# Attention normalizations, residual, input sums and chunk sums on GpSimd, and 29 mixed experts in 16 slots

## The chip, the cores and the metric

The kernel runs on one core of one Trainium2 chip. The metric is the time of one execution on the device, in microseconds (us); smaller is better. Before the change the median of three runs is 3224.7 us (3222.76 to 3225.04).

A core has five engines, each with an instruction stream that it takes in order: TensorE (PE: matrix products and transposes; its weight loads are listed as PEld), VectorE (DVE), ScalarE (ACT), GpSimd (POOL) and SyncE (SP, which in this kernel issues all data transfers). They wait for each other by semaphores. PE writes to PSUM, a small memory of eight banks that DVE and ACT read. In this kernel GpSimd works on SBUF alone, the larger on-chip memory.

## What is computed

Two layers over x of shape (4, 2048, 512), all in float32: a windowed attention (16 heads of width 32; a window of 128 queries looks at the keys of the window before, its own and the one after), then a feed-forward layer whose weights are mixed from 8 experts, one mix for each of the 4 sequences. Cut to what matters:

```python
x = x + layernorm(attention(layernorm(x), w_qkv))
x = x + layernorm(ffn(layernorm(x), ...))

def ffn(x):                                        # E = 8 experts, F = 2048, H = 512
    h = relu(einsum('bsh,oh->bso', x, gate_w1) + gate_b1)
    g = (einsum('bso,eo->bse', h, gate_w2) + gate_b2).mean(axis=1)
    mW1 = W1 + einsum('be,efh->bfh', g, TW1)       # the mixing
    mW2 = W2 + einsum('be,ehf->bhf', g, TW2)
    mb1, mb2 = b1 + g @ Tb1, b2 + g @ Tb2
    u = gelu(einsum('bsh,bfh->bsf', x, mW1) + mb1[:, None, :])
    return einsum('bsf,bhf->bsh', u, mW2) + mb2[:, None, :]
```

The gate g of a sequence is a mean over the whole sequence, so its weights can be mixed only when the attention has passed all of it.

## The kernel before

The order of all work is written out by hand; no scheduler moves anything. There are two stages.

**Attention.** 64 windows (W_) of 128 rows, 4 groups of heads (g) for each: 256 slots, slot i being window i // 4, group i % 4. A block K is four windows, 512 rows. One slot issues, in this order (the loop at line 962):

- `scores(i + 1)`: 8 products of q and k (L649) for the slot after, and on DVE two reductions for the negated row maxima `nm` (L658);
- `turn(i, j)`: 12 transposes of the probabilities `pr` on PE (L686), copied out of PSUM by ACT to `prT` (L691). The banks for them (`ptp`) are three that rotate under the tag "pt"; whatever transposes come next (`pto`, `ptx`) take the bank that the first copy has set free;
- `mid[i]`: in slots with i % 4 == 1 the attention output of the window before is transposed back (`pto`, L311), scaled by DVE (L316, L318) and its mean and variance taken (`stats`: L92 and L94 on DVE, then L96 and L98, two small operations on GpSimd). In slots with i % 4 == 0 the normalized second input `xn2` is transposed (`ptx`, L340);
- `exponentials(i + 1)` on ACT (L671), which need `nm`;
- `dense[i]`: a part of the q, k, v or gate products for a later block (L518), with Strassen-Winograd's seven products in place of eight. `pair_read` and `gate_read` take the sums out of PSUM, on DVE (L546, L548, L781 to L792) or ACT;
- `rest[i]`: among others `residual` at i % 4 == 2 (normalize the attention output, add x, take statistics, store to `x1_d`), `norm_stats` of a later input tile and `normed` at i % 4 == 3, `norm_tile` at i % 4 == 0, and `right_factors` in slots with i % 16 of 0, 1 (projections) and 12, 13 (gate): four sums of quarters of the input, 128x512 each, needed by `dense` one to three slots later;
- from slot 85 on, `MIXED[i % 16]` steps of the mixer;
- the other read of `dense`, then every second slot `values` (L707, probabilities times v), then `late[i]`.

The slots repeat with a period of 16: twelve for one block's projections and four for a gate. `a`, `x1` and `xn2` of a window are one tile in SBUF, overwritten in place; two windows have one each.

**The mixer** (line 106) is a generator. 64 chunks (4 sequences, W1 and W2, 8 chunks each) of 8 experts. A step loads the expert three ahead (512 KB; four buffers, `exps`) and adds one expert with its gate to the chunk's accumulator on DVE (L155). After a chunk's eighth expert, one more step makes four sums of its quarters on DVE (L163 to L166, 128x256 each), which are Strassen's left factors; its store to memory is issued in the step after, on SP. `MIXED` adds up to 21 steps in 16 slots.

**Feed-forward.** 16 blocks K of 512 rows. For a block 4 sets of first products (28 matmuls of 128x128 by 256 for a set, L1023, with ACT's gelus and DVE's sums) and 7 second products (L1143; in the last sequence a second level of Strassen, L1308). The steps of the mixer that are left are taken here, at counts written out for each block, until the mixer is empty; it must be empty by the end of block 11's sets.

The change touches `normalize`, `mixer`, `gate_end`, `residual`, `normed`, `norm_tile`, `right_factors`, the lists of `rest` and `late`, `MIXED` and the slot loop.

Of the kernel before, what the change touches and what calls it, by code (L numbers as in the profile page):

```python
# [34 lines left out]
def sandwich(ctx: ExitStack, tc: tile.TileContext, x, w_qkv, gw1, gb1, gw2, gb2, w1, b1, w2, b2, tw1, tb1, tw2, tb2, out):  # L35
# [65 lines left out]
    def normalize(dst, src, sm):  # L101
        mv, rs = sm
        nc.vector.tensor_scalar(dst, src, mv[:, 0:1], rs, ALU.subtract, ALU.mult)


    def mixer():
# [41 lines left out]
        for n, (b, s, c, e) in enumerate(todo):  # L148
# [5 lines left out]
            acc = accs[b, s, c]  # L154
            nc.vector.scalar_tensor_tensor(acc, ets.pop(n), g_all[b][:, e : e + 1], acc, ALU.mult, ALU.add)  # L155
            yield
            if e == NX - 1:
# [5 lines left out]
                nc.vector.tensor_tensor(sums[:, 0, :], a21, a22, ALU.add)  # L163
                nc.vector.tensor_tensor(a21, a11, a21, ALU.subtract)
                nc.vector.tensor_tensor(sums[:, 1, :], sums[:, 0, :], a11, ALU.subtract)
                nc.vector.tensor_tensor(sums[:, 2, :], a12, sums[:, 1, :], ALU.subtract)  # L166
                late.append(lambda b=b, s=s, c=c, acc=acc, sums=sums: store(b, s, c, acc, sums))
                yield
# [92 lines left out]
    def gate_end(b, hsum, bank, spare):  # L261
# [24 lines left out]

        def first_biases():
# [38 lines left out]
    def residual(W_):  # L326
        st = win[W_]
        x1 = st["x1"]
        normalize(x1, st["a"], st["sb"])
        nc.vector.tensor_tensor(x1, x1, st["x"], ALU.add)  # L330
        nc.sync.dma_start(x1_d[W_], x1)
        st["sc"] = stats(x1, f"c{W_}")

    def normed(W_):
        st = win[W_]
        normalize(st["xn2"], st["x1"], st["sc"])
# [58 lines left out]
    with ExitStack() as actx:  # L395
# [39 lines left out]
        def norm_tile(K, t):  # L435
            xn = xn_of[K, t] = x_of.pop((K, t))
            normalize(xn, xn, xs_of.pop((K, t)))
# [36 lines left out]
        def right_factors(K, part, i=0):  # L474
# [255 lines left out]
        for K in range(1, NBK):  # L730
            s0 = 4 * (4 * K - 5)
            if K > 1:
                for t in range(WB):
# [4 lines left out]
                    rest[i + 1].append(lambda K=K, t=t: norm_tile(K, t))  # L738
# [116 lines left out]
        for W_ in range(NWA - 1):  # L855
# [3 lines left out]
            rest[i + 1].append(lambda W_=W_: residual(W_))  # L859
            rest[i + 2].append(lambda W_=W_: normed(W_))  # L860
# [69 lines left out]
        for t in range(WB):  # L930
            x_of[1, t] = load_tile(1, t, "x", 4)
        load_rest()
        right_factors(0, 0)
# [5 lines left out]
            (1, 2): [lambda: right_factors(0, 1)],  # L939
# [22 lines left out]
        for i in range(NS):  # L962
# [22 lines left out]
            if i >= 85:  # L985
                for _ in range(MIXED[i % 16]):
                    next(blend)
# [617 lines left out]
```

## Time and profile before

| what | value |
| --- | --- |
| median of three runs | 3224.7 us |
| the profiled execution, its own time | 3224.83 us |
| its span, first to last instruction | 3223.0 us |
| PE busy | 3197.1 us |
| DVE busy | 2278.8 us, 3307 instructions |
| ACT busy | 1576.5 us |
| GpSimd busy | 676.5 us, 847 instructions |
| granted TensorE clock | 0.998 |
| one expert (L155), 512 of them | 697.1 us, 1362 ns each |
| normalizations (L103), 128x512 | 538, 537 and 532 ns each |
| residual sum (L330), 63 of them | 692 ns each |
| a chunk's four sums (L163 to L166) | 532, 484, 468 and 517 ns |
| right_factors' four sums (L482, L483, L486, L487) | 681, 692, 661 and 685 ns |

The attention lasts from the start to about 1661 us, the feed-forward from there to the end. Busy time is what an engine worked, not what it delayed: whether an engine matters is read from what PE waits for. A table of windows gives, for a stretch of the span, each engine's busy time with the number of instructions in brackets. A timeline line gives start, duration, engine, source line, operation, output and inputs; in brackets stands how long the engine was idle before, and what ended that.

### The profile page before, as it was taken

How to read it: one execution, taken by the hardware profiler on the slowest of the kernel's cores; microseconds unless marked ns; L12 is line 12 of the kernel's file. 1: busy time of each engine (PE TensorE's matmuls, PEld its weight loads, DVE VectorE, ACT ScalarE, POOL GpSimd, SP SyncE). 2: the span in 40 equal slices, each digit the busy share in tenths (PEclk: the TensorE clock that was granted, in tenths of full speed). 3: DMA queues.
4: the chain of work that ended last, by engine and by line, in shares of the span. 5: the costliest groups of instructions: out<-in, count | busy, mean ns of one | idle time of the engine just before them, and what ended most of it. 6: DMA issues, size and time to landing. Idle time of an engine off the chain costs nothing.

```text
span 3223.0 us, 61653 instructions
## 1 busy us (share of the span) xinstructions
PE 3197.1 (99%) x23862; PEld 2697.0 (84%) x23862; DVE 2278.8 (71%) x3307; ACT 1576.5 (49%) x4332; POOL 676.5 (21%) x847
## 2 busy tenths in 40 slices
PE   9999999999999999999999999999999999999998
PEld 7788888888788888878768888888888888889998
DVE  5766666888998889888865665677657667554555
ACT  3777777777777777777761222112222112222222
POOL 0111111111111111110112322323322323332233
PEclk9999999999999999999999999999999999999999
DMA  2111112455555556554677889999899999874555
GB/s 87 54 57 54 40 60 80 138 189 163 193 193 168 178 177 200 194 174 151 211 277 277 310 309 345 355 337 330 311 330 361 341 326 322 305 246 155 193 187 170
DMA packets 363334, 688.88 MB, mean 214 GB/s; under 512 B 27161, under 2 KB 115353, under 8 KB 357026
## 3 DMA queue, kind: packets, MB, share of 16 engines
q1 hardware_dynamic: 363042, 684.94, 61.4%
q8 instruction: 189, 3.10, 0.4%
q14 instruction: 103, 0.84, 0.1%
HBM read 567.39 MB, written 117.44 MB: 212 GB/s over the span
## 4 chain that ended last, share of the span: by engine, by line
PE 94%; DVE 2%; DMA 2%; ACT 1%; POOL 0%; issue 0%; SPq 0%; POOLq 0%; DVEq 0%; ACTq 0%
PE pm L518 23%; PE px L1023 13%; PE ptp L686 11%; PE px L1143 7%; PE sc L649 7%; PE pz L1023 6%; PE po L707 5%; PE pz L1143 5%; PE py L1023 3%; PE py L1143 3%; PE px L1308 2%; PE py2b L1143 2%; PE pz L1308 1%; PE pm L582 1%; PE ptx L340 1%; PE pto L311 1%
## 5 line engine op out<-in xcount | busy, mean ns | idle before, releaser
L155 DVE SCALAR_TENSOR_TENSOR acc<-exps,g,acc 128x1024 f32<-128x1024 f32 x512 | 697.1, 1362 | 66.1 <-DMA exps<-in_tw 60.1
L658 DVE TENSOR_REDUCE nm<-sc 128x2 f32<-128x768 f32 (+1 forms) x512 | 449.2, 918 | 206.8 <-PE sc L649 201.8
L671 ACT ACTIVATE pr<-sc,nm 128x384 f32<-128x384 f32 (+1 forms) x1024 | 572.8, 592 | 11.3 <-DVE nm L658 11.1
L691 ACT COPY prT<-ptp 128x512 f32<-128x512 f32 x732 | 382.9, 595 | 281.3 <-PE ptp L686 281.1
L686 PEld LDWEIGHTS ptp<-ident,pr 128*128 128x128 f32 x2944 | 318.0, 141 | 102.3 <-issue 89.8
L686 PE MATMUL ptp<-ident,pr 128*128 128x128 f32 x2944 | 378.7, 278 | 0.0
L1060 ACT COPY py<-px 128x512 f32<-128x512 f32 x63 | 36.0, 571 | 662.6 <-PE px L1023 662.4
L1023 PE MATMUL px<-tT,w 128*128 128x256 f32 x1512 | 350.1, 379 | 0.6 <-DVE cpv L1083 0.6
L1023 PEld LDWEIGHTS px<-tT,w 128*128 128x128 f32 x1512 | 286.9, 190 | 40.0 <-DVE cpv L1083 1.0
L649 PE MATMUL sc<-k,q 32*128 32x384 f32 (+2 forms) x2816 | 243.2, 423 | 3.7 <-ACT pr L671 3.5
L671 ACT ACTIVATION_READ_ACCUMULATOR pr<-sc,nm 128x1 f32 x1024 | 236.5, 231 | 0.0
L1080 DVE TENSOR_TENSOR cpb<-pz,cpb 128x512 f32<-128x512 f32 x63 | 43.4, 689 | 268.8 <-PE pz L1023 240.1
L96 POOL TENSOR_SCALAR ve_b<-mv_b 128x1 f32<-128x1 f32 x64 | 42.8, 669 | 819.2 <-DVE mv_b L94 819.2
L707 PEld LDWEIGHTS po<-prT,v 128*32 128x32 f32 x5888 | 152.2, 110 | 50.9 <-ACT pr L671 25.4
L707 PE MATMUL po<-prT,v 128*32 128x128 f32 x5888 | 189.7, 275 | 0.2
L649 PEld LDWEIGHTS sc<-k,q 32*128 32x128 f32 x2816 | 118.7, 184 | 74.4 <-issue 53.9
L1143 PE MATMUL px<-w2s,u 128*128 128x256 f32 x784 | 175.1, 379 | 0.0
L518 PE MATMUL pm<-xnT,wqkv 128*128 128x256 f32 x720 | 172.2, 382 | 0.0
L1105 POOL TENSOR_TENSOR t<-u 128x512 f32<-128x512 f32 x60 | 79.9, 1332 | 434.8 <-ACT u L1035 434.8
L1143 PEld LDWEIGHTS px<-w2s,u 128*128 128x128 f32 x784 | 149.0, 190 | 20.2
L518 PEld LDWEIGHTS pm<-xnT,wqkv 128*128 128x128 f32 x720 | 132.0, 190 | 16.7
L1074 ACT COPY cpb<-px 128x512 f32<-128x512 f32 x63 | 36.9, 585 | 182.0 <-PE px L1023 182.0
(295 smaller groups left out, 5911.6 us busy)
## 6 DMA issues: line engine op xcount, KB each, us to landing
exps<-in_tw SPq DMA_DIRECT2D x512, 512.0 KB, 6.0
w2s<-m2d SPq DMA_DIRECT2D x168, 512.0 KB, 8.1
w2s<-m3d SPq DMA_DIRECT2D x84, 512.0 KB, 4.7
acc<-in_w SPq DMA_DIRECT2D x64, 512.0 KB, 6.1
x<-in_x SPq DMA_DIRECT2D x64, 256.0 KB, 4.2
m1d<-acc SPq DMA_DIRECT2D x64, 256.0 KB, 6.3
w<-m1d SPq DMA_DIRECT2D x16, 1024.0 KB, 7.9
fxT<-xTd SPq DMA_DIRECT2D x16, 1024.0 KB, 8.5
```

Source lines behind the costliest of these rows:

```text
L155: nc.vector.scalar_tensor_tensor(acc, ets.pop(n), g_all[b][:, e : e + 1], acc, ALU.mult, ALU.add)
L518: nc.tensor.matmul(bank[u not in chain][:, half, :], lhsT=a[:, kc, ts(half, P)], rhs=b[:, kc, :], start=(u not in (2, 3, 4) and half == kc ...
L649: nc.tensor.matmul(scs[r // 2][:, r % 2, col : col + nj * W], lhsT=q[rows, g, ts(W_ % WB, W)], rhs=k_of[kb][rows, g, j0 * W : (j0 + nj) * ...
L658: nc.vector.tensor_reduce(st["nm"][:, h : h + 2], scs[u][:, :, : nk * W], AX.X, ALU.max, negate=True)
L671: nc.scalar.activation(pr[:, : nk * W], scs[r // 2][:, r % 2, : nk * W], AF.Exp, bias=st["nm"][:, h : h + 1], accum_out=st["den"][:, h : h ...
L686: nc.tensor.transpose(pt[:, r, :], st["pr"][g * 4 + r][:, ts(j, W)], ident)
L691: nc.scalar.copy(prT, pt)
L707: nc.tensor.matmul(po[r * E : (r + 1) * E, n, :], lhsT=v_of[kb][:, jj, h * E : (h + 1) * E], rhs=prT[:, r, :], start=(j == 0), stop=(j == ...
L1023: nc.tensor.matmul(bank[:, f, :], lhsT=factor[:, f, kc * P : (kc + 1) * P], rhs=right[:, kc, :], start=(start and f == 0 and kc == 0), sto ...
L1105: nc.gpsimd.tensor_tensor(t1s[c], b12, us[c][:, :, :Q], ALU.subtract)
L1143: nc.tensor.matmul(bank[:, t, :], lhsT=right(c - c % 2)[:, c % 2, ts(t, P)], rhs=w[:, c % (HC // 2), :], start=(start and c == 0 and t == ...
L1308: nc.tensor.matmul(bank, lhsT=right(p), rhs=w[:, p, :], start=(start and p == 0), stop=True, skip_group_check=True,)
```

## The change

- `normalize` gets an engine; `residual`'s normalization and sum, `normed`, the input tiles' `norm_tile` in the slots, and `right_factors` in the slots go from DVE to GpSimd. In the last window (after the slots) and in the start-up they stay on DVE.
- `residual` is split: the store to `x1_d` and the statistics of x1 become `residual_stats`, which stands in `late` of the same slot.
- While the attention runs, a chunk's four sums go to GpSimd and are no step of their own: they are issued in the step of the eighth expert.
- `MIXED` adds up to 29, and as no step is a sum any more, 29 experts in 16 slots. Where it says 3, the third expert comes after the second read of `dense`.
- `gated` only asserts that a sequence's gate is made before it is mixed.

```diff
-    def normalize(dst, src, sm):
+    def normalize(dst, src, sm, engine=nc.vector):
         mv, rs = sm
-        nc.vector.tensor_scalar(dst, src, mv[:, 0:1], rs, ALU.subtract, ALU.mult)
+        engine.tensor_scalar(dst, src, mv[:, 0:1], rs, ALU.subtract, ALU.mult)
+
+    attending, gated = [True], set()
...
                 sums = mix.tile([P, 3, Q], F32, tag="sums", bufs=1, name=f"sums_{b}_{s}_{c}")
-                nc.vector.tensor_tensor(sums[:, 0, :], a21, a22, ALU.add)
-                nc.vector.tensor_tensor(a21, a11, a21, ALU.subtract)
-                nc.vector.tensor_tensor(sums[:, 1, :], sums[:, 0, :], a11, ALU.subtract)
-                nc.vector.tensor_tensor(sums[:, 2, :], a12, sums[:, 1, :], ALU.subtract)
+                engine = nc.gpsimd if attending[0] else nc.vector
+                engine.tensor_tensor(sums[:, 0, :], a21, a22, ALU.add)
+                engine.tensor_tensor(a21, a11, a21, ALU.subtract)
+                engine.tensor_tensor(sums[:, 1, :], sums[:, 0, :], a11, ALU.subtract)
+                engine.tensor_tensor(sums[:, 2, :], a12, sums[:, 1, :], ALU.subtract)
                 late.append(lambda b=b, s=s, c=c, acc=acc, sums=sums: store(b, s, c, acc, sums))
-                yield
+                if not attending[0]:
+                    yield
...
-    def residual(W_):
+    def residual(W_, engine=nc.gpsimd):
         st = win[W_]
         x1 = st["x1"]
-        normalize(x1, st["a"], st["sb"])
-        nc.vector.tensor_tensor(x1, x1, st["x"], ALU.add)
-        nc.sync.dma_start(x1_d[W_], x1)
-        st["sc"] = stats(x1, f"c{W_}")
-
-    def normed(W_):
+        normalize(x1, st["a"], st["sb"], engine)
+        engine.tensor_tensor(x1, x1, st["x"], ALU.add)
+
+    def residual_stats(W_):
         st = win[W_]
-        normalize(st["xn2"], st["x1"], st["sc"])
+        nc.sync.dma_start(x1_d[W_], st["x1"])
+        st["sc"] = stats(st["x1"], f"c{W_}")
+
+    def normed(W_, engine=nc.gpsimd):
+        st = win[W_]
+        normalize(st["xn2"], st["x1"], st["sc"], engine)
...
-        def right_factors(K, part, i=0):
+        def right_factors(K, part, i=0, engine=nc.gpsimd):
...
-                nc.vector.tensor_tensor(t[:, 0], r12, r11, ALU.subtract)
-                nc.vector.tensor_tensor(t[:, 1], r22, t[:, 0], ALU.subtract)
+                engine.tensor_tensor(t[:, 0], r12, r11, ALU.subtract)
+                engine.tensor_tensor(t[:, 1], r22, t[:, 0], ALU.subtract)
...
-                nc.vector.tensor_tensor(r12, r22, r12, ALU.subtract)
-                nc.vector.tensor_tensor(t["T4"], r21, t["T2"], ALU.subtract)
+                engine.tensor_tensor(r12, r22, r12, ALU.subtract)
+                engine.tensor_tensor(t["T4"], r21, t["T2"], ALU.subtract)
...
-                    rest[i + 1].append(lambda K=K, t=t: norm_tile(K, t))
+                    rest[i + 1].append(lambda K=K, t=t: norm_tile(K, t, nc.gpsimd))
...
             rest[i + 1].append(lambda W_=W_: residual(W_))
+            late[i + 1].append(lambda W_=W_: residual_stats(W_))
             rest[i + 2].append(lambda W_=W_: normed(W_))
...
-        MIXED = (1, 0, 1, 1, 2, 1, 1, 2, 2, 1, 1, 1, 2, 1, 2, 2)
+        MIXED = (2, 1, 1, 3, 2, 1, 1, 3, 2, 1, 1, 3, 2, 2, 1, 3)
...
             if i >= 85:
-                for _ in range(MIXED[i % 16]):
+                for _ in range(min(2, MIXED[i % 16])):
                     next(blend)
             if dense[i]:
                 dense[i][1]()
+            if i >= 85 and MIXED[i % 16] > 2:
+                next(blend)
             for f in behind[i]:
                 f()
...
+    attending[0] = False
...
-            ("set", 1): [lambda: residual(last)],
-            ("set", 2): [lambda: normed(last)],
+            ("set", 1): [lambda: residual(last, nc.vector), lambda: residual_stats(last)],
+            ("set", 2): [lambda: normed(last, nc.vector)],
```

More of the change, by code (lines that the diff above doesn't have):

```diff
@@ L154, in mixer @@
             acc = accs[b, s, c]
+            assert b in gated
             nc.vector.scalar_tensor_tensor(acc, ets.pop(n), g_all[b][:, e : e + 1], acc, ALU.mult, ALU.add)
@@ L285, in experts @@
             nc.vector.tensor_copy(gcb[:NX, :], gc.to_broadcast([NX, P]))
+            gated.add(b)
         def first_biases():
@@ L433, in norm_stats, with norm_tile @@
             xs_of[K, t] = stats(x_of[K, t], f"a{K}_{t}")
-        def norm_tile(K, t):
+        def norm_tile(K, t, engine=nc.vector):
             xn = xn_of[K, t] = x_of.pop((K, t))
-            normalize(xn, xn, xs_of.pop((K, t)))
+            normalize(xn, xn, xs_of.pop((K, t)), engine)
         def place_tile(K, t, evac, then=None):
@@ L932, in sandwich @@
         load_rest()
-        right_factors(0, 0)
+        right_factors(0, 0, engine=nc.vector)
         left_factors(0)
@@ L938, in sandwich @@
             (1, 1): [lambda: left_factors(2)],
-            (1, 2): [lambda: right_factors(0, 1)],
+            (1, 2): [lambda: right_factors(0, 1, engine=nc.vector)],
             (2, 2): [lambda: norm_stats(1, 0), lambda: norm_stats(1, 1)],
```

## The prediction

> **What bounds the kernel now.** I read the chain of waits first: it names PE for nearly all of the span. The slices above it say that DVE is at nine tenths in the second half of the attention, so the next question is whether PE ever waits for DVE there.
>
> ```profile
> DVE  5766666888998889888865665677657667554555
> ...
> PE 94%; DVE 2%; DMA 2%; ACT 1%; POOL 0%; issue 0%; SPq 0%; POOLq 0%; DVEq 0%; ACTq 0%
> ```
>
> The table of windows answers it. Its first two lines are the same 16 slots of two sequences, one without and one with mixing; the other two are a block of the feed-forward each (columns: stretch, its length, busy time with count for PE, PEld, DVE, ACT, POOL, then clock, DMA share, GB/s).
>
> ```profile
> 445.30:544.70 99.40, 99.40 (x953) 80.38 (x948) 64.10 (x104) 73.18 (x218) 11.62 (x24) 1.00 0.18 57
> 854.90:954.30 99.40, 99.40 (x953) 80.39 (x950) 90.34 (x132) 73.18 (x218) 13.54 (x24) 1.00 0.59 196
> 2061.70:2158.40 96.70, 96.70 (x450) 85.14 (x449) 69.59 (x81) 22.47 (x48) 29.66 (x30) 1.00 0.93 334
> 2255.10:2351.80 96.70, 96.70 (x450) 85.14 (x449) 66.33 (x77) 22.55 (x48) 30.10 (x29) 1.00 0.91 326
> ```
>
> 26 us more of DVE work cost the 16 slots nothing: 99.40 us both times. And 450 feed-forward matmuls take 96.70 us in either block, 215 ns each, back to back. PE sets the pace of both stages. What DVE is relieved of can't shorten them; what makes DVE late can lengthen them. So the price of this change is read from how late DVE may be in a slot.
>
> That is in the timeline of a slot with i % 4 == 3 (from 727.12) and the two after it (from 732.99 and 739.46):
>
> ```profile
> 727.12 0.95 PE L649 MATMUL sc<-k,q 32*128 32x256 f32 x16
> 728.11 1.82 DVE L658 TENSOR_REDUCE nm<-sc 128x2 f32<-128x768 f32 x2 [1.00 <-PE sc L649]
> 729.85 0.69 DVE L92 BATCH_NORM_STATS2 st_a<-x 128x6 f32<-128x512 f32 x1
> 730.67 0.53 DVE L103 TENSOR_SCALAR x<-x,mv_c,rs_c 128x512 f32<-128x512 f32 x1
> 731.36 0.57 POOL L98 TENSOR_TENSOR rs_a<-ve_a,mhalf 128x1 f32<-128x1 f32 x1
> 731.37 0.69 DVE L548 TENSOR_TENSOR v<-pm,v 128x512 f32<-128x512 f32 x1 [0.17 <-PE pm L518]
> 731.98 1.27 DVE L155 SCALAR_TENSOR_TENSOR acc<-exps,g,acc 128x1024 f32<-128x1024 f32 x1
> 732.99 0.96 PE L649 MATMUL sc<-k,q 32*128 32x256 f32 x16
> 733.98 1.82 DVE L658 TENSOR_REDUCE nm<-sc 128x2 f32<-128x768 f32 x2 [0.72 <-PE sc L649]
> 736.01 0.61 ACT L671 ACTIVATE pr<-sc,nm 128x384 f32<-128x384 f32 x1
> 741.05 1.57 ACT L691 COPY prT<-ptp 128x512 f32<-128x512 f32 x3 [0.88 <-PE ptp L686]
> 741.72 0.62 PE L311 MATMUL pto<-ident,oT 128*128 128x128 f32 x4
> ```
>
> The first reduction ends at about 734.93 (half of 1.82 after 733.98, plus a start-up), the exponential that needs it starts at 736.01: ACT comes 1.08 us later anyway. ACT then works without a gap until its copy at 741.05, before which it idles 0.88. The copy frees the bank for `pto`: its first third ends near 741.65, PE starts at 741.72. So this `nm` may be 1.08 + 0.88 = 1.96 us late; each further microsecond stops PE. (For the transposes of `pr` themselves the room is larger.)
>
> **The change part by part.** *DVE's average.* In 16 slots it loses 12 normalizations (6.4 us at 0.53), 4 residual sums (2.8 at 0.69), 8 input sums (5.4 at 0.68) and, as 21 steps are 18.7 experts and 2.3 chunks' sums, these sums (4.0; 1.7 us a chunk in the attention's timeline), 18.6 us in all; it gains 29 - 18.7 = 10.3 experts at 1.28 = 13.2. From 90.3 it comes to 85 of 99.4. By itself this is worth nothing, since PE wasn't waiting.
>
> *DVE's peak.* Slots with i % 4 == 3 now take three experts where this one took one. Losing L103 doesn't help there: the next instruction, L548, waits for PE until 731.37 in any case. So three experts start at 731.98 and end, at 1.295 each in a row (a pair elsewhere takes 2.59), at 735.86; the next `nm` can start 1.88 us late instead of on time. That alone is 0.08 below the limit of 1.96.
>
> *What GpSimd does at that moment.* By the order of its instructions, after `rs_a` (which ends at 731.93) come the window's `normed` and the input tile's `norm_tile`. They are ready as the first expert starts, and they read SBUF while L155 reads two SBUF operands. That pair is in the trace, in the feed-forward:
>
> ```profile
> 2117.75 3.51 DVE L155 SCALAR_TENSOR_TENSOR acc<-exps,g,acc 128x1024 f32<-128x1024 f32 x2
> 2118.92 1.27 POOL L1181 TENSOR_TENSOR t<-u,t 128x512 f32<-128x512 f32 x1 [6.85 <-PE pz L1143]
> ```
>
> Two experts take 3.51 us in place of 2.59 when one 128x512 GpSimd sum comes between them: 0.92 us of delay. No GpSimd normalization of 512 columns is in the trace. Below, the 128x1 tensor_scalar rows (0.22 to 0.67 us, L96) delay DVE by nothing that I can find; above, the sum's 0.92. A normalization reads one operand, the sum two: I take half, 0.46 (the row it is nearest to is the sum), with 0 and 0.92 as ends. Two of them: 1.88 + 0.92 - 1.96 = 0.84 us of PE a burst. There are 43 such slots from 87 to 255; `norm_tile` ends at slot 220, so 34 bursts have both (28.6 us) and 9 only `normed` (0.38 each, 3.4 us). In slots with i % 16 == 15 the slot is 0.5 longer, but the first input sum (0.92) comes into the burst in place of one normalization (0.46): same price.
>
> *Chunk sums on GpSimd.* Four operations of 256 columns, by half of 1.27 plus a start some 0.7 each. A chunk ends 0.91 times in four slots; with 7.25 experts in these, 2 of 7.25 ends fall on the first or second expert of a burst, a quarter of the bursts. Then one or two more operations at 0.46 come between experts: 43 x 0.25 x 0.69 = 7.4 us. The others run beside `nm`, which reads PSUM.
>
> *Input sums.* In the 9 slots with i % 16 == 11 the gate's first sums are ready early, and I give half of them a third place in the burst: 9 x 0.46 = 4.1 us. For PE the tightest is T3, the third sum: GpSimd gets to it after `rs_b`, 6.6 us into its slot by the trace; with 1.3 us it is done some 2 us into the next, where PE needs it after 4. Hidden, unless chunk sums (2.8 us) stand in front: then up to 1 us is lost, in few periods; 0 here.
>
> *Residual.* `rs_b` ends as slot i % 4 == 2 begins; normalization and sum (about 0.8 + 1.3) are done 2.5 us into a slot of 7.3 us, long before DVE reaches `residual_stats`: no wait, so nothing behind it (the next `nm`) is late. On SP the store to `x1_d` now stands after the experts' loads of its slot; what is queued behind it, the next experts, are loaded three ahead. `normed` overwrites the tile that this store reads: landing takes 2.3 us (median), done before the burst. The chunk's store waits for four GpSimd operations and holds SP some 3 us; loads land 4.8 us after issue and four buffers cover some 13 us (four at 99.4 / 29). Cost 0; if that cover went, the fourth and fifth expert of a burst would wait.
>
> *Feed-forward.* 310 experts are mixed in the attention in place of 201, so the mixer is empty in block 7 and not 11. From the first product of block 1 (1768.6) to that of block 12 (2836.2) are 1067.6 us, 11 blocks at 96.7 make 1063.7: at most 3.9 us to win, of which 0.9 lies in blocks 8 and 10. I take -0.9.
>
> *Sum.* 28.6 + 3.4 + 7.4 + 4.1 - 0.9 = 42.6 us on the span of 3223.0: 3265.6. That execution took 3224.83, 1.8 more than its span and 0.1 more than the median: 3267.
>
> *The skill.* The Trainium skill, SBUF — State Buffer, section "Who interferes with whom", says that a DVE instruction with two SBUF inputs and a GpSimd instruction that reads SBUF exclude each other, the later one waiting until the first is finished; the trace agrees in kind, with 0.92 us for an operation of 1.27. Its GPSIMD Engine Reference, "Engine selection", speaks against the change: elementwise work belongs on VectorE, two-input operations being about twice as slow on GpSimd, one-input ones near line rate. An estimate from that page's 769 ns for 512 elements, all of it blocking, would be 1.54 in place of 0.92 a burst, some 21 us more.
>
> **Rivals.** *No change:* GpSimd finds no turn between experts in a row, or its two normalizations come after the burst, beside `nm`. It decides if two cost under 0.08 us together; then bursts stay within 1.96 and PE keeps its pace: 3224 to 3226. For it: 1.88 is below 1.96, and DVE's average falls. Against it: 3.51 against 2.59, and `rs_a` ending just as the burst starts.
> *Faster:* the feed-forward, free of mixing and its loads from block 8 on, loses all its waits: -3.9, 3221. For more than that there is no row: 215 ns a matmul is the same with every load on DVE.
> *GpSimd falls behind:* its 16 slots hold 12 normalizations at 0.8, 12 sums at 1.27, 14.5 at 0.7 and 13.5 us of small operations, 49 of 99 us; waits for DVE come on top. If T3 or `normed` is late for PE by 2 us once in 16 slots, 11 periods cost 20 us more: 3287.
>
> **How the numbers follow.** Forecast 3267, chance 0.64; GpSimd behind 0.12; no change 0.18; faster 0.06, half of it by more than 0.2%, which is about what a measurement of this kernel can tell from no change (6.4 us). Upper end with 0.92 a normalization: 1.76 x 34 + 0.84 x 9 + 7.4 + 4.1 - 0.9 = 78, 3303. Lower end with 0: bursts cost nothing, chunk and input sums some 11 us, 3236; to leave out no more than 2 in 10 the range goes down to the no-change case: 3222 to 3303. The likeliest case's own range is 3236 to 3303. Faster 0.03, same 0.21, slower 0.76.
>
> **What would show it.** Right: the second slot after each burst is longer by 0.4 to 1.7 us than before, with ACT's `pr` waiting for DVE's `nm` and the copy before `pto` without idle time; L155's longest instances near 1.8 to 2.2 us in the attention; feed-forward blocks at 96.7. Wrong: 16 slots still at 99.40 us, or the lost time at other slots, with PE waiting for GpSimd's `tx` or for `xn2`, or DVE for `exps`.

## The result, and the profile after

The changed kernel takes 3317.1 us (median of four runs, 3315.4 to 3323.5) against 3224.5 for the kernel before beside it: 1.0292 times the time, 95% interval 1.0274 to 1.0310. The profiled execution took 3323.45 us, its span is 3321.7, 98.7 more than before; its line numbers from the mixer on are 3 to 14 higher than before (`sc` L659, `nm` L668, `pr` L681, the expert L158, the chunk's sums L167 to L170, the residual's sum L337, the store to `x1_d` L341).

The page of the changed kernel, its slices, its chain of waits and the costliest row of GpSimd:

```profile
DVE  5555455788788887888864666576663211254555
...
POOL 1544454567666776766544232233222222222223
...
PE 82%; DVE 6%; POOL 5%; DMA 4%; issue 1%; ACT 1%; SPq 0%; POOLq 0%; DVEq 0%; ACTq 0%
...
L103 POOL TENSOR_SCALAR x<-x,mv_c,rs_c 128x512 f32<-128x512 f32 x63 | 143.1, 2271 | 29.9 <-DMA x1d<-x 26.0
```

DVE's share falls from nine tenths to about eight in the mixing part and GpSimd's rises to six or seven. But the stage has become longer: in the mean of nine periods of 16 slots (of 102.4 us before, 110.0 after) DVE is busy for 91.6 us, against 90.9 before. PE's share of the chain has fallen from 94% to 82%, and DVE, GpSimd and DMA now hold 15% together. One normalization of 128x512 takes GpSimd 2.09 us with no expert beside it and 2.27 on average in this row; it took DVE 0.53.

The added time lies in the attention: to the last `sc` it is 1749.4 us, 88.2 more than before. By slots (each compared with the same slot before): 34.5 us in the second slots after a burst of three experts (i % 4 == 1), 20.7 in the first (i % 4 == 0), 10.4 in the third, 4.0 in the burst's own, 6.1 before any mixing, 12.3 in the last 16 slots. Another 9.6 us lie between the last `sc` and the first feed-forward product, and 0.9 in the feed-forward, whose blocks are what they were (windows of the changed kernel, columns as before):

```profile
2064.10:2160.80 96.70, 96.70 (x449) 85.13 (x449) 57.60 (x66) 22.54 (x48) 28.02 (x28) 1.00 0.91 345
```

**A burst** is what the prediction described. The timeline of slot 167 and the one after:

```profile
1163.64 2.09 POOL L103 TENSOR_SCALAR x<-x,mv_c,rs_c 128x512 f32<-128x512 f32 x1
...
1163.93 4.59 DVE L158 SCALAR_TENSOR_TENSOR acc<-exps,g,acc 128x1024 f32<-128x1024 f32 x3
...
1164.94 0.93 PE L659 MATMUL sc<-k,q 32*128 32x384 f32 x8
...
1165.72 3.04 POOL L103 TENSOR_SCALAR x<-x,mv_a,rs_a 128x512 f32<-128x512 f32 x1
...
1168.44 1.81 DVE L668 TENSOR_REDUCE nm<-sc 128x2 f32<-128x768 f32 x2
1169.48 0.58 ACT L681 ACTIVATE pr<-sc,nm 128x384 f32<-128x384 f32 x1 [1.43 <-DVE nm L668]
...
1170.97 1.84 PE L659 MATMUL sc<-k,q 32*128 32x384 f32 x8
...
1171.89 0.30 PEld L659 LDWEIGHTS sc<-k,q 32*128 32x128 f32 x4 [0.63 <-ACT pr L681]
```

One normalization starts just before the burst and one within it, and the burst takes 4.59 us (a bare burst, shown below, 3.92). The reduction `nm` starts 3.50 us after its `sc` instead of 0.96, so 2.54 late; `pr` waits for it, and the next slot's scores take 1.84 us instead of 0.93, because their second half (the last line) waits for `pr` to free its bank. That slot is 0.92 us longer. Where nothing else disturbs them, such bursts cost 0.91 to 0.93 with both normalizations; with `normed` alone (the last 36 slots) 0.46 and 0.49 occur. Many others cost less: over all 34 bursts that have both, with the lumps of the next paragraph, the mean is 0.96, and 0.59 in a later kernel without those lumps ("the three parts that were priced at nothing").

**The lumps** are the other half: 17 slots between 85 and 239 lose over 1.25 us each, 43 us together. Two of them, 1.8 us and right behind it the largest, 6.6, are in this timeline (DVE, GpSimd, PE's `sc` and `ptx`, and SP's issues):

```profile
867.46 2.17 POOL L496 TENSOR_TENSOR gT<-gT 128x512 f32<-128x512 f32 x1
...
869.60 1.26 POOL L497 TENSOR_TENSOR tx_True<-gT,tx_True 128x512 f32<-128x512 f32 x1
...
870.82 0.72 POOL L167 TENSOR_TENSOR sums<-acc 128x256 f32<-128x256 f32 x1
...
874.06 0.72 POOL L170 TENSOR_TENSOR sums<-acc,sums 128x256 f32<-128x256 f32 x1
874.77 2.08 POOL L103 TENSOR_SCALAR x<-x,mv_b,rs_b 128x512 f32<-128x512 f32 x1
874.81 0.37 SPq L144 DMA_DIRECT2D m2d<-sums  x1
...
876.94 1.27 POOL L337 TENSOR_TENSOR x<-x,xr 128x512 f32<-128x512 f32 x1
...
878.24 0.69 DVE L92 BATCH_NORM_STATS2 st_c<-x 128x6 f32<-128x512 f32 x1 [4.93 <-POOL x L337]
...
879.82 0.47 ACT L681 ACTIVATE pr<-sc,nm 128x256 f32<-128x256 f32 x1 [3.95 <-DVE nm L668]
...
880.89 0.70 PE L659 MATMUL sc<-k,q 32*128 32x256 f32 x4 [1.74 <-ACT pr L681]
...
883.41 2.78 POOL L103 TENSOR_SCALAR x<-x,mv_c,rs_c 128x512 f32<-128x512 f32 x1 [1.32 <-DMA x1d<-x]
...
886.24 1.12 PE L350 MATMUL ptx<-ident,x 128*128 128x128 f32 x4 [1.32 <-POOL x L103]
```

Two input sums, a chunk's four sums and only then the residual: its inputs are ready at 867.5, it is done at 878.2. DVE has reached `residual_stats` at 873.3 and stands still for 4.93 us; the `nm` of the next scores is queued behind it, `pr` waits 3.95 for that, and PE 1.74 at a stretch. This slot (873.45 to 880.89) is 1.8 us longer than before. On SP the chunk's store waited for the sums until 874.8, and the store to `x1_d` is issued at 878.2. It lands late, so in the slot after (880.89 to 892.36) `normed`, which overwrites the tile that this store reads, waits 1.32 us for it, and PE waits as long for `normed`. These waits are the smaller part of that slot's 6.6 us: for 10.2 us of it the granted clock is 0.50 (see "Why the prediction was off").

### The profile page after: what moved, and what is told of

The parts are those of the page before. It is cut to its first block, busy times and chain, and to the rows that moved or that the text cites. A ratio compares the mean times of both kernels' runs of the same rounds, so it can differ in the third digit from the quotient of the medians.

```text
span 3321.7 us, 61902 instructions
## 1 busy us (share of the span) xinstructions
PE 3253.0 (98%) x23862; PEld 2724.2 (82%) x23862; DVE 2055.1 (62%) x2794; ACT 1582.3 (48%) x4332; POOL 1480.5 (45%) x1360
## 4 chain that ended last, share of the span: by engine, by line
PE 82%; DVE 6%; POOL 5%; DMA 4%; issue 1%; ACT 1%; SPq 0%; POOLq 0%; DVEq 0%; ACTq 0%
PE pm L528 17%; PE px L1037 13%; PE ptp L696 8%; PE px L1157 7%; PE pz L1037 6%; PE sc L659 5%; PE pz L1157 5%; PE po L717 4%; PE py L1037 3%; PE py L1157 2%; PE px L1322 2%; PE py2b L1157 2%; DVE acc L158 2%; POOL x L103 2%; DVE nm L668 1%
## 5 line engine op out<-in xcount | busy, mean ns | idle before, releaser
L158 DVE SCALAR_TENSOR_TENSOR acc<-exps,g,acc 128x1024 f32<-128x1024 f32 x512 | 731.1, 1430 | 92.2 <-DMA exps<-in_tw 85.5
L681 ACT ACTIVATE pr<-sc,nm 128x384 f32<-128x384 f32 (+1 forms) x1024 | 571.7, 587 | 97.7 <-DVE nm L668 97.5
L668 DVE TENSOR_REDUCE nm<-sc 128x2 f32<-128x768 f32 (+1 forms) x512 | 448.2, 916 | 173.6 <-PE sc L659 168.5
L696 PE MATMUL ptp<-ident,pr 128*128 128x128 f32 x2944 | 386.8, 282 | 0.1
L659 PE MATMUL sc<-k,q 32*128 32x384 f32 (+2 forms) x2816 | 269.7, 424 | 23.8 <-ACT pr L681 23.3
L681 ACT ACTIVATION_READ_ACCUMULATOR pr<-sc,nm 128x1 f32 x1024 | 231.2, 226 | 0.0
L659 PEld LDWEIGHTS sc<-k,q 32*128 32x128 f32 x2816 | 130.8, 184 | 108.6 <-issue 52.4
L96 POOL TENSOR_SCALAR ve_d<-mv_d 128x1 f32<-128x1 f32 x62 | 19.3, 311 | 393.9 <-DVE mv_d L94 393.9
L103 POOL TENSOR_SCALAR x<-x,mv_c,rs_c 128x512 f32<-128x512 f32 x63 | 143.1, 2271 | 29.9 <-DMA x1d<-x 26.0
```

The costliest lines, as they stand in the source:

```text
L103: engine.tensor_scalar(dst, src, mv[:, 0:1], rs, ALU.subtract, ALU.mult)
L659: nc.tensor.matmul(scs[r // 2][:, r % 2, col : col + nj * W], lhsT=q[rows, g, ts(W_ % WB, W)], rhs=k_of[kb][rows, g, j0 * W : (j0 + nj) * ...
L668: nc.vector.tensor_reduce(st["nm"][:, h : h + 2], scs[u][:, :, : nk * W], AX.X, ALU.max, negate=True)
L681: nc.scalar.activation(pr[:, : nk * W], scs[r // 2][:, r % 2, : nk * W], AF.Exp, bias=st["nm"][:, h : h + 1], accum_out=st["den"][:, h : h ...
L696: nc.tensor.transpose(pt[:, r, :], st["pr"][g * 4 + r][:, ts(j, W)], ident)
```

## Experiments

All times are medians of four runs, ratios against the kernel before on the same chip, with 95% intervals. Differences between two changed kernels are differences of such medians, often from two chips; on these the kernel before took 3223.9 to 3226.0 us. Each "Theory" is explained in the expectation that names it first. Losses by slots are from one profiled execution of each kernel.

### The normalizations back on DVE

```diff
-        normalize(x1, st["a"], st["sb"], engine)
+        normalize(x1, st["a"], st["sb"])
...
-        normalize(st["xn2"], st["x1"], st["sc"], engine)
+        normalize(st["xn2"], st["x1"], st["sc"])
...
-                    rest[i + 1].append(lambda K=K, t=t: norm_tile(K, t, nc.gpsimd))
+                    rest[i + 1].append(lambda K=K, t=t: norm_tile(K, t))
```

> The three normalizations (input tile, residual, second input) are on VectorE again; the residual's sum, the input sums, the chunk sums and 29 experts in 16 slots stay as changed. Theory 1 (the normalizations on GpSimd take 2.09 us each, come between the experts of a burst and make GpSimd late): most of the 92.6 us goes, 3225 to 3250 us. Theory 2 (three experts in one slot make VectorE late whatever GpSimd does): little goes, 3285 to 3320 us.

Measured: 3320.6 us, 1.0302 (1.0285 to 1.0319), just above Theory 2's range. Theory 1 falls as it stands: GpSimd loses its 2.09 us operations and nothing is won. Only the 6.1 us before the mixing go (0.6 left). The residual's sum is still on GpSimd, now between two DVE operations, and 20 slots still lose over 1.25 us.

### The rate of before, the moves of the change

```diff
-        MIXED = (2, 1, 1, 3, 2, 1, 1, 3, 2, 1, 1, 3, 2, 2, 1, 3)
+        MIXED = (1, 0, 1, 1, 2, 1, 1, 2, 2, 1, 1, 1, 2, 1, 2, 2)
```

> The changed kernel with MIXED of before, 21 steps in 16 slots and no slot with three. Theory 1: GpSimd's load is nearly the same, and PE still waits for xn2 and for statistics that wait for GpSimd: 3245 to 3280 us. Theory 2: without bursts of three PE keeps its pace, 3223 to 3235 us.

Measured: 3244.7 us, 1.0062 (1.0047 to 1.0077), at the low end of Theory 1's range and above Theory 2's. The moves cost some 20 us without any burst, at 21 experts in 16 slots (the kernel before mixes 18.7): 6.2 before the mixing, 10 in four lumps. The other 72 come only with the change's 29 and its bursts.

### 29 experts spread out

```diff
-        MIXED = (2, 1, 1, 3, 2, 1, 1, 3, 2, 1, 1, 3, 2, 2, 1, 3)
+        MIXED = (2, 2, 2, 1, 2, 2, 2, 1, 2, 2, 2, 1, 2, 2, 2, 2)
```

> The changed kernel with 29 experts in 16 slots laid out as 2, 2, 2, 1 (the last four 2, 2, 2, 2): one expert where the change has three, two where it has one. The same GpSimd work and the same number of experts. Theory 1: the experts still meet GpSimd, at other places, and GpSimd is as late: 3280 to 3320 us. Theory 2: 3225 to 3250 us.

Measured: 3345.3 us, 1.0378 (1.0363 to 1.0394), slower still, and above both ranges. The second slots lose 2.5 us in place of 34.5, so the bursts' loss is gone; the slots i % 4 == 0, where `ptx` needs `xn2`, lose 74.2 in place of 20.7, where PE waits 54.5 us (26 times) for GpSimd's `xn2`. Why `xn2` comes so much later when the experts are spread was not separated further.

### The statistics a slot later

```diff
-            late[i + 1].append(lambda W_=W_: residual_stats(W_))
-            rest[i + 2].append(lambda W_=W_: normed(W_))
+            rest[i + 2].append(lambda W_=W_: residual_stats(W_))
+            late[i + 2].append(lambda W_=W_: normed(W_))
```

> The changed kernel with the statistics of x1 and its store moved one slot later, into the rest of that slot, and normed to the end of it, so that VectorE doesn't stand waiting for GpSimd's residual sum at the end of a slot. Theory 3 (VectorE's wait for that sum, 33.6 us in the changed kernel's trace, with the row maxima queued behind it, is a large part): 3270 to 3295 us. Theories 1 and 2: 3300 to 3325 us, as the normalizations and bursts stay and xn2 gets less time.

Measured: 3415.2 us, 1.0589 (1.0573 to 1.0604), far above both ranges. The wait that this takes from DVE comes back as PE's: `normed` starts later, and the slots with `ptx` lose 153 us. So this run can't price DVE's wait for the residual; taking the residual from GpSimd does (below).

### The chunk's sums back on DVE

```diff
-                engine = nc.gpsimd if attending[0] else nc.vector
+                engine = nc.vector
```

> The changed kernel, but the chunk's four sums are on DVE again in the attention (still without a step of their own). Theory 4, GpSimd's queue: the chunk's sums (some 4 us of GpSimd with 256 columns each) stand ahead of the residual and of the input sums, and SP, waiting for them in front of the chunk's store, holds the loads and stores behind it (its waits for sums were 93 and 70 us in all). Without them GpSimd is never far behind: the lumps of 4 to 18 us go, only the regular loss of 4 us in 16 slots stays: 3250 to 3285 us. Theory 5, DVE's own load: at 29 experts in 16 slots DVE has no room left for any wait; with 3.6 chunks x 1.7 us = 6 us more in 16 slots it gets worse or stays: 3310 to 3340 us.

Measured: 3341.3 us, 1.0358 (1.0343 to 1.0374). Theory 4 falls for the sums, and Theory 5's range is missed by 1 us: of the moves that were undone one by one this is the only one that pays at 29 experts in 16 slots, 24 us.

### The chunk's store three experts later

```diff
-            for f in late:
-                f()
-            late = []
+            while late and late[0][0] <= n:
+                late.pop(0)[1]()
...
-                late.append(lambda b=b, s=s, c=c, acc=acc, sums=sums: store(b, s, c, acc, sums))
+                late.append((n + (4 if attending[0] else 1), lambda b=b, s=s, c=c, acc=acc, sums=sums: store(b, s, c, acc, sums)))
```

> The changed kernel, but in the attention a chunk's store is issued three experts later, when GpSimd's sums of it are done, so that SP isn't held in front of it. Theory 4: the part of the loss that goes through SP's queue (x1's store late, so its tile is late to be overwritten, and experts' loads late: DVE waited 41 us for exps, GpSimd 26 us for the store) goes: 3280 to 3305 us. Theory 5: DVE is as loaded as before; 3312 to 3325 us.

Measured: 3306.8 us, 1.0252 (1.0237 to 1.0267): 10.3 us less, just above the top of Theory 4's range and outside Theory 5's. In the changed kernel SP stood still before those stores (its own waits: what is issued, what it waits for, us in total, times, longest):

```profile
SPq L341 <- POOL x L337: 145.3, 36, 7.8
SPq L133 <- POOL sums L169: 92.7, 19, 10.9
SPq L144 <- POOL sums L170: 70.1, 12, 12.2
```

With the later store DVE's waits for experts fall from 40.9 us to 10.0.

### The input sums back on DVE

```diff
-        def right_factors(K, part, i=0, engine=nc.gpsimd):
+        def right_factors(K, part, i=0, engine=nc.vector):
```

> The changed kernel, but the input sums (two of 128x512 in each of two slots of 16, and T4 and T3) are on DVE again. Theory 4: GpSimd has 4 x 1.27 us less in 16 slots for each set, just where the largest lump (6.6 us in slot 128) stood: the lump there goes, the chunk's sums still come ahead of the residual elsewhere: 3285 to 3305 us. Theory 5: DVE has 5.4 us more in 16 slots: 3315 to 3345 us.

Measured: 3298.9 us, 1.0225 (1.0210 to 1.0240): 18.2 us less though DVE has more to do. Theory 4 holds here: 8 slots lose over 1.25 us in place of 17, the slot of 6.6 us now loses 2.8 (its clock stays at 1.00), and DVE waits 20.6 us for the residual in place of 35.2.

### The rate alone, nothing moved

The kernel before, with:

```diff
-                yield
+                if not attending[0]:
+                    yield
...
-        MIXED = (1, 0, 1, 1, 2, 1, 1, 2, 2, 1, 1, 1, 2, 1, 2, 2)
+        MIXED = (2, 1, 1, 3, 2, 1, 1, 3, 2, 1, 1, 3, 2, 2, 1, 3)
...
-                for _ in range(MIXED[i % 16]):
+                for _ in range(min(2, MIXED[i % 16])):
                     next(blend)
             if dense[i]:
                 dense[i][1]()
+            if i >= 85 and MIXED[i % 16] > 2:
+                next(blend)
```

> The kernel before, with nothing moved to GpSimd, and only the mixing of the change (29 experts in 16 slots, no step for the sums, the third expert behind the second read). It prices the rate without GpSimd. DVE's sum for 16 slots is 90.3 + 10.3 x 1.28 + 1.3 chunks x 1.7 = 105.7 us of 99.4. If DVE's own sum is what decides (Theory 5), each of 10.7 periods is 6.3 us longer or more: 3290 to 3330 us, so moving the work to GpSimd gave DVE nothing in the end. If DVE's waits for GpSimd and SP are what made the changed kernel slow (Theory 4), this kernel has none of them: 3230 to 3290 us, faster than the changed one.

Measured: 3301.5 us, 1.0237 (1.0220 to 1.0254), within Theory 5's range. Its page shows a DVE that is full:

```profile
DVE  5766666999999999999985666667653221354555
```

Over nine periods DVE idles 5.0 us in 109.7. In the changed kernel it idles 18.4 in 110.0: the same period, made of waits. The moves take 13.1 us of work from DVE in each period (104.8 to 91.6 us busy), and all of it comes back as idle time. So from slot 85 to 239 the moves make next to no difference, 69.5 us lost with them and 65.9 without; what they add to the whole, 15.6 us (3317.1 against 3301.5), lies mostly outside: before the mixing, in the last 16 slots and behind the attention.

### Bursts of three at the rate of before

The kernel of "the rate alone", and then the changed kernel, each with:

```diff
-        MIXED = (2, 1, 1, 3, 2, 1, 1, 3, 2, 1, 1, 3, 2, 2, 1, 3)
+        MIXED = (1, 1, 1, 3, 1, 0, 1, 3, 1, 0, 1, 3, 1, 0, 1, 3)
```

> The kernel before, nothing moved to GpSimd, with 21 steps in 16 slots as before, but three of them together in each fourth slot (and the chunk's sums without a step of their own, so 21 experts, about 2.3 more than before). It tells a burst of three from the rate. By the prediction's own arithmetic three experts in a row make the next nm 1.88 us late, under the limit of 1.96: 3225 to 3229 us. If three together are what costs (Theory 2: 37 us of loss lay in the second slots after the bursts at 29 in 16, with or without the moves): 43 bursts at 0.5 to 1 us, 3245 to 3270. If DVE's sum is what decides (Theory 5; here 90.3 + 2.3 x 1.28 + 0.3 x 1.7 = 93.8 of 99.4): 3225 to 3230.

> The changed kernel with all its moves, with the same 21 in bursts of three. By the prediction's arithmetic the two normalizations of GpSimd come between the experts of a burst and cost 0.84 x 34 + 0.38 x 9 = 32 us more than the same kernel with 21 spread out (3244.7): 3277. By Theory 5 (DVE has room again) 3240 to 3255, as with 21 spread out.

Measured: 3273.0 us, 1.0150 (1.0135 to 1.0165), and with the moves 3278.3, 1.0167 (1.0152 to 1.0182). The second lands on the number of the prediction's arithmetic, 3277. The first is 3 us above Theory 2's range and far from the prediction's arithmetic: nothing is moved to GpSimd, and it costs 49 us all the same. The timeline of the first shows why:

```profile
794.47 2.60 DVE L157 SCALAR_TENSOR_TENSOR acc<-exps,g,acc 128x1024 f32<-128x1024 f32 x2
797.10 0.42 DVE L165 TENSOR_TENSOR sums<-acc 128x256 f32<-128x256 f32 x1
...
798.35 0.42 DVE L168 TENSOR_TENSOR sums<-acc,sums 128x256 f32<-128x256 f32 x1
798.69 1.28 DVE L157 SCALAR_TENSOR_TENSOR acc<-exps,g,acc 128x1024 f32<-128x1024 f32 x1
799.89 1.82 DVE L661 TENSOR_REDUCE nm<-sc 128x2 f32<-128x768 f32 x2
```

A chunk's four sums, no longer a step of their own, stand inside the burst: 1.7 us more before `nm`. This burst costs 1.9 us (0.78 and 1.11 in two slots); a burst without sums costs 0.31. The next run takes the sums out of the bursts.

### The bare burst

The kernel of "the rate alone" with that MIXED, and of the moves the chunk's sums on GpSimd with the later store:

```diff
-                nc.vector.tensor_tensor(sums[:, 0, :], a21, a22, ALU.add)
+                engine = nc.gpsimd if attending[0] else nc.vector
+                engine.tensor_tensor(sums[:, 0, :], a21, a22, ALU.add)
...
-        MIXED = (2, 1, 1, 3, 2, 1, 1, 3, 2, 1, 1, 3, 2, 2, 1, 3)
+        MIXED = (1, 1, 1, 3, 1, 0, 1, 3, 1, 0, 1, 3, 1, 0, 1, 3)
```

> 21 in 16 slots in bursts of three, nothing on GpSimd but the chunk's sums with their store three experts later. It prices the bare burst of three experts. In burst21 the slots two after a burst were 0.31 us longer where no chunk ended in it, and 1.9 (0.78 + 1.11) where one did, with its four sums of 0.42 in the burst. So if the sums were the cost: 43 x 0.31 = 13 us, 3234 to 3245. If the burst itself is: near burst21, 3260 to 3275.

Measured: 3246.0 us, 1.0068 (1.0053 to 1.0083), 1 us above the range of "the sums were the cost". A bare burst:

```profile
1128.33 3.92 DVE L156 SCALAR_TENSOR_TENSOR acc<-exps,g,acc 128x1024 f32<-128x1024 f32 x3
1129.34 0.31 PEld L652 LDWEIGHTS sc<-k,q 32*128 32x128 f32 x8 [0.33 <-issue]
1129.34 0.93 PE L652 MATMUL sc<-k,q 32*128 32x384 f32 x8
...
1132.16 1.81 DVE L661 TENSOR_REDUCE nm<-sc 128x2 f32<-128x768 f32 x2
1133.21 0.58 ACT L674 ACTIVATE pr<-sc,nm 128x384 f32<-128x384 f32 x1 [0.75 <-DVE nm L661]
...
1135.29 0.63 PEld L652 LDWEIGHTS sc<-k,q 32*128 32x128 f32 x8 [0.20 <-issue]
1135.29 1.24 PE L652 MATMUL sc<-k,q 32*128 32x384 f32 x8
```

`nm` starts 2.82 us after its `sc` instead of 0.96: 1.86 late. The scores that follow take 1.24 us instead of 0.93, and that slot is 0.31 longer.

### 29 with only the chunk's sums moved, in bursts and spread

The kernel of "the rate alone" with the chunk's sums on GpSimd and the later store; first with the change's MIXED, then with:

```diff
-        MIXED = (2, 1, 1, 3, 2, 1, 1, 3, 2, 1, 1, 3, 2, 2, 1, 3)
+        MIXED = (2, 2, 2, 1, 2, 2, 2, 1, 2, 2, 2, 1, 2, 2, 2, 2)
```

> The kernel before with the mixing of the change (29 in 16 slots), and of the moves only the chunk sums on GpSimd, with their store three experts later so that SP isn't held. DVE's sum falls from 105.7 to 99.6 us in 16 slots. Theory 5, DVE's sum decides at 29: 6.1 x 10.7 = 65 us less than with all on DVE (3301.5): 3236 to 3270. If the bursts decide (Theory 2), their loss stays: 3280 to 3300.

> 29 in 16 slots spread as 2, 2, 2, 1, with nothing on GpSimd but the chunk's sums and their store later: the kernel that ran at 3272 with bursts, without them. If the bursts decide (Theory 2): 3225 to 3250. If DVE's sum decides (99.6 us of 99.4 in 16 slots, 5 us idle only): 3260 to 3290.

Measured: 3272.1 us, 1.0148 (1.0131 to 1.0165), just above the top of Theory 5's range, and 3261.0, 1.0114 (1.0099 to 1.0129), Theory 5's low end. Without bursts 37 us remain, and DVE, busy for 100.3 us, idles 5.3 in a period of 105.6 (102.4 before): by these numbers 29 experts are more than DVE has room for even without the sums. The bursts add 11.

### The residual whole on DVE

```diff
-    def residual(W_, engine=nc.gpsimd):
+    def residual(W_, engine=nc.vector):
...
-            late[i + 1].append(lambda W_=W_: residual_stats(W_))
+            rest[i + 1].append(lambda W_=W_: residual_stats(W_))
```

> The changed kernel, but the residual is whole on DVE again, its normalization and its sum, with the store and the statistics right behind them; the other normalizations, the input sums and the chunk sums stay on GpSimd. Theory 3: DVE's waits for GpSimd's residual sum (35 us in 22 waits) and the lumps behind them (17 losses of over 1.25 us, 43 us in all) go, against 4 x 1.22 = 4.9 us more of DVE in 16 slots, which it has in its 18 us of idle time: 3270 to 3300. Theory 5: DVE's sum decides, 4.9 us x 10.7 periods on top, less what the waits cost: 3315 to 3340.

Measured: 3303.4 us, 1.0245 (1.0230 to 1.0261): 13.7 less than the changed kernel, 3 above Theory 3's range and well below Theory 5's. DVE's wait for the residual costs more than the 4.9 us of work in 16 slots that the move takes from it.

### The three parts that were priced at nothing, undone together

```diff
-    def residual(W_, engine=nc.gpsimd):
+    def residual(W_, engine=nc.vector):
...
-            late[i + 1].append(lambda W_=W_: residual_stats(W_))
+            rest[i + 1].append(lambda W_=W_: residual_stats(W_))
...
-        def right_factors(K, part, i=0, engine=nc.gpsimd):
+        def right_factors(K, part, i=0, engine=nc.vector):
...
-                late.append(lambda b=b, s=s, c=c, acc=acc, sums=sums: store(b, s, c, acc, sums))
+                late.append((n + (4 if attending[0] else 1), lambda b=b, s=s, c=c, acc=acc, sums=sums: store(b, s, c, acc, sums)))
```

> The changed kernel with three of its parts undone together: the residual whole on DVE, the input sums on DVE, and the chunk's store three experts later. On GpSimd stay the two normalizations that fall into the bursts and the chunk's sums; the mixing stays at 29 in 16 slots with its bursts. These three are what the prediction priced at nothing. If they are the missing 50 us (each alone gave 14, 18 and 10 us): 3267 to 3280, the forecast's own sum. If it is DVE's sum that decides (Theory 5: DVE gets 10.3 us more in 16 slots): above 3300.

Measured: 3275.9 us, 1.0162 (1.0145 to 1.0179), within the range for "the missing 50 us": 41.2 us less, and the three alone gave 13.7 + 18.2 + 10.3 = 42.2. They add up. Four slots lose over 1.25 us in place of 17. The slices of its page:

```profile
DVE  5655566899999999999874676667653211354555
...
POOL 0323222344545444443333222233322222322223
```

No wait of DVE for GpSimd's residual is left, and its waits for experts fall from 40.9 to 8.3 us. SP still waits for the store to `x1_d`, now for DVE's sum (210.6 us in 42 waits), more than the 145.3 us in the changed kernel: that SP stands still costs nothing by itself, only when what stands behind it is due.

This kernel has a twin among the runs above: "29 with only the chunk's sums moved, in bursts" differs from it only in that `normed` and the input tiles' `norm_tile` are on DVE. The twin takes 3272.1 us, 1.0148 (1.0131 to 1.0165), against 3275.9 here. The intervals overlap, and the mean loss in the second slot after a burst, over the 34 bursts that have both normalizations here, is 0.59 us here and 0.57 in the twin. So with the three parts undone, moving the two normalizations to GpSimd costs some 4 us net or nothing.

## Why the prediction was off

What held. PE sets the pace of the kernel before, and the feed-forward doesn't move (0.9 us more, where 0.9 less was forecast). The loss of a burst is where the prediction put it, in the second slot after, by `nm` being late, with GpSimd's two normalizations between the experts. Where nothing else disturbs it, it is near the forecast price, too: 0.92 measured against 0.84 with both, 0.46 against 0.38 with one. That nearness is luck in part, as its terms were off in opposite directions. Three experts make `nm` 1.86 late (1.88 forecast). The two normalizations delay this burst by 4.59 - 3.92 = 0.67 us, 0.33 each (0.46 forecast); over the 16 bursts of the changed kernel that have both, with no sum of GpSimd beside them, it is 4.48 on average, 0.28 each. The limit isn't 1.96: what PE meets first isn't the bank for `pto` but the second half of the next `sc`, whose bank `pr` frees, and from 1.86 late and 0.31 lost, or 2.54 and 0.92, it is 1.55 to 1.6. So a bare burst isn't free, as forecast, and a good part of the forecast's 32 us for the normalizations is lost without them: the twin of the last experiment shows a net price of some 4 us for moving them. Their delay of the experts is there, and DVE is relieved of the same work; the runs show only what is left of both.

What failed is three zeros and the duration behind them.

- *"no wait, so nothing behind it is late"* (the residual). It stood on "about 0.8 + 1.3" us for GpSimd's normalization and sum. No run shows the 0.8: the normalization is 2.09 us by itself, and other work stands in front of it. DVE waited 22 times for the residual, 35.2 us in all, longest 4.9, with `nm` behind. Undone: 13.7 us. The page of the Trainium skill that the prediction cites, GPSIMD Engine Reference, "Engine selection", has one-input operations near line rate and two-input ones at half. The trace agrees for the sum (1.27 us against DVE's 0.69) and not for this normalization, which subtracts and multiplies with two scalars per partition from SBUF (2.09 against 0.53).
- *"Hidden, unless chunk sums stand in front: then up to 1 us is lost, in few periods; 0 here"* (input sums). The chunk's sums did stand in front, and what the input sums delay isn't only T3 but the residual behind them in GpSimd's queue (DVE's wait for it falls from 35.2 to 20.6 us when they go). Undone: 18.2 us.
- *"Cost 0; if that cover went, the fourth and fifth expert of a burst would wait"* (the chunk's store on SP). The hold was forecast at 3 us; it was up to 12.2, as SP waits for all that GpSimd has in front of the sums. The cover went: DVE waited 40.9 us for experts, GpSimd 26.0 for the store to `x1_d`. Undone: 10.3 us.

The three undone together give 41.2 us, of the 50 by which the forecast was too low. The rival "GpSimd falls behind" was this, with the right sign at 20 us beside the forecast; it belonged in the sum, and twice as large. It took 49 of 99 us for GpSimd's load; the mean of nine periods of the changed kernel is 74.2 of 110.0. *DVE's average*, forecast to fall from 90.3 to 85 us in 16 slots, didn't fall: in the mean of nine periods it is 90.9 before and 91.6 after. One reason is that an expert takes 1428 ns on average in the attention instead of 1277, as GpSimd's operations come between, 4.4 us for 29. And relief of DVE, "worth nothing" in the forecast, is worth something at the new rate: with 29 experts in 16 slots, taking the chunk's sums from it gains 24 us.

Another cost was in no case: PE's own clock. The first three windows of the changed kernel hold the period of the lump, ten microseconds after its wait, and the eight after that; the fourth is behind the attention. Below stand two groups of matmuls of the same shape, 128x256, one in the second window and one in the 20 us behind it (busy, mean ns):

```profile
873.50:989.40 115.90, 109.43 (x954) 86.14 (x950) 89.30 (x109) 73.92 (x217) 76.92 (x63) 0.94 0.70 234
...
881.80:892.00 10.20, 8.88 (x51) 6.55 (x55) 8.80 (x7) 5.52 (x17) 8.80 (x5) 0.50 0.82 281
892.10:900.00 7.90, 7.90 (x66) 6.22 (x59) 5.96 (x10) 5.41 (x19) 4.09 (x5) 1.00 0.70 243
...
1759.10:1769.30 10.20, 5.10 (x14) 4.28 (x15) 2.73 (x3) 0.58 (x1) 2.52 (x1) 0.50 0.53 162
```

```profile
L528 PE MATMUL pm<-xnT,wqkv 128*128 128x256 f32 x8 | 3.6, 634 | 0.0
```

```profile
L528 PE MATMUL pm<-tx_False,wsum 128*128 128x256 f32 x16 | 3.7, 384 | 0.0
```

After PE's pause of 1.7 us the granted clock falls to 0.50 for 10.2 us and a matmul takes 634 ns instead of 384; eight of them take 3.6 us, where at clock 1.00 sixteen take 3.7. Over the whole span PE is busy for 50.4 us at half clock, against 3.4 before. If the 47 us more would take half as long at full clock, some 23 of the 98.7 us are lost to the clock (an estimate from these rows). This doesn't come on top of the losses counted by slots but lies within them: the 17 lumps hold 27 us of half clock, the slot of 6.6 us alone 10.2. The 9.6 us before the feed-forward are of this kind, too: PE waits 6.7 us for the last `xn2`, during which the clock falls, and then works its first 5.1 us at half of it.

What stays open. The kernel with the three zeros undone is at 3275.9, near the forecast of 3267, but that is luck in part, since its loss isn't made up as the forecast's was. There, 39 us were for the bursts with their normalizations and chunk sums. Measured are 21 us in the second slots after bursts, 10 in the first, 7 in the last 16 slots and 6 behind the attention; the twin without the normalizations loses 48 of the 52 us, and 29 experts without bursts or normalizations on GpSimd lose 37. So most of what is left comes with the rate of 29, which the forecast put at nothing; that this is DVE's sum alone is argued from its 5 us of idle time in a period, not shown. No version was faster than the kernel before; PE is busy for nearly all of that one's span, and the feed-forward held at most 3.9 us.

## What to carry to other kernels

Before work is moved to an idle engine, add up that engine's queue in order, with its own durations for the very operation, and follow who waits for each result, through the DMA queue too: here a GpSimd that idled a third of the time made DVE, SP and PE wait, because an urgent residual stood behind sums, some of which nobody needed soon. In these runs the move paid whose result had slack (the chunk's sums, 24 us), and those cost whose result was due soon or that stood in front of one (the residual and the input sums, 14 and 18 us), whatever they took off the busy engine. And a busy engine that isn't waited for at one rate of work can be at the next: 29 experts in 16 slots cost 77 us with nothing moved, and 37 spread out with only the chunk's sums moved. A zero in a sum needs the same working as the other terms: what has to stay true for it, and what it costs when it doesn't.

## What the hardware showed that was not expected

- A GpSimd normalization of 128x512 (subtract, then multiply, with one scalar of each per partition) took 2.09 us (2.08 to 2.10 with no expert beside it), longer than its sum of two 128x512 operands, 1.27. Yet each of two delayed a burst of experts by only 0.28 us on average, where the sum in the feed-forward delayed a pair by 0.92; beside experts the normalization itself was stretched, to 3.0 us in the burst shown and 3.6 at most.
- The granted clock fell to 0.5, mostly for 3.4 us or two or three times that, after short pauses of PE. Counted over the attention of all 17 profiled kernels (a pause runs from the end of a matmul or weight load to the start of the next), pauses of 0.6 to 1.29 us were followed by such a fall within 6 us 22 times of 122, of 1.29 to 2 us 37 times of 63, of 2 to 3.4 us 30 of 37, above that 34 of 34. That is an order in time, not an experiment: the pauses were not set one by one, several can stand before one fall, and the kernels share much of their timeline. The Trainium skill, TensorE: Matmul & The Clock Gate, "HAM oscillation — how this bites in real kernels", warns of idle gaps above some 3.4 us; here more than half of the pauses between 1.29 and 2 us were followed by a fall. By an estimate from the 3.4 to 10.2 us at half clock, a wait of 1.7 us can cost PE another 1.7 to 5.1.
